# Router logits, places and masked context in quadrants of 32 result rows, in a fused cross-attention and mixture-of-experts kernel on one core

## The chip, the core and the metric

The kernel runs on one core of a Trainium2 chip. A core has a matrix engine (TensorE, PE in the profile, with its weight loads shown apart as PEld), a vector engine (DVE), a scalar engine (ACT), a general engine (POOL) and a queue processor (SP) that issues transfers. Matrix products land in PSUM, from where DVE or ACT copies them on. The metric is device time in microseconds (us) of one execution; lower is better. All data are 32-bit floats.

## What is computed

The input is 64 batches of 128 tokens of width 128, and for each batch a context of 77 rows of width 96. Two residual blocks follow each other:

```python
x = x + tanh(g_xattn[0]) * xattn(layernorm(x), ctx, mask)   # 16 heads of 8, softmax over 77 context rows
x = x + tanh(g_ffn[0])   * ffn(layernorm(x))

# ffn: 8 experts, 2 of them per token
gate_scores = softmax(x @ Wg)                      # Wg: 128 x 8, the router
topk_scores, topk_idx = top_k(gate_scores, 2)
topk_scores = topk_scores / (topk_scores.sum(-1) + 1e-8)
fused = gate * sigmoid(gate) * value               # gate = x @ W11[e], value = x @ W12[e], 128 -> 256
expert_out = fused @ W2[e]                         # 256 -> 128
out = sum of topk_scores * expert_out over the two experts
```

The kernel doesn't compute all eight experts for every token. It sorts the tokens by expert: each token's row is written to DRAM at a place that belongs to its expert, and the expert stage then works through tiles of 128 rows with one expert each.

## The kernel before

**Attention.** The 64 batches are taken in 16 groups of four (`G = 4`). A main loop runs over items `i`, one per batch: `scores` of batch `i`, `turn` (transposes of the score differences and their exponentials) of batch `i - 1`, `values` of a batch further on, `mix` (the sums over the context) of batch `i - 2`, `turn_last` of batch `i - 1`. Around these pieces each item has two slots, PRE (ahead of the scores) and POST (behind `turn_last`). The steps that belong to a whole group are placed in these slots by hand: the table `AT` gives each step's item relative to the group's first batch, and the order in which instructions are written is the order on PE, ACT, DVE and POOL (`tc.manual_schedule`). SP's transfers are outside of it.

Three of these steps are touched by the change:

- `context_t` (L520, at item -7, POST): per batch the product of the context (77 rows x 96 columns, the stationary operand) with `sel`, a 77 x 77 matrix that masks rows out. The result `pc` has 96 rows and 4 x 77 columns. ACT copies it out as `cT` (L527) and partly as `czs` (L529). On PE it stands between `tl` (the transposes of `turn_last`, L895) and `pt_a`, the transposes of the normalised tokens (L389), which the next item's scores (`sc`, L860) follow.
- `logits` (L635, at item 13, PRE): per batch the product of the transposed tokens (128 x 128, stationary) with `wg` (128 x 8). The result `pg` has 128 rows and 4 x 8 columns. DVE reads it twice, as `gm` and `gp` (L644, L646).
- `places` (L698, at item 17, PRE): two products accumulated in one result `pp` of 128 x 32: `earlier` (a triangle of ones, 128 x 128, stationary) with the group's choices `both`, and `ones` (128 x 128, stationary) with the running counts. They give each token its place within its expert's region. DVE turns this into `place` (L708), `at`, `to` and `dest` (L717), and POOL uses `dest` in the group's eight dispatches (L722): indirect transfers of 128 rows each, two of them directly after the item's scores and the others in the next items' slots. Items 13 and 17 differ by one group, so `places` of group g - 1 and `logits` of group g come in the same slot, one behind the other, ahead of that item's scores. In most groups `pk`, the keys product of a later group (L544), stands just before them.

Results of most products share a ring of three PSUM buffers (`product`, L382). A product that takes a buffer must wait until its last result has been read. As the program is built, in the items with places and logits the places take the buffer of `po` (the mix, read by ACT as `os` and `lz`, L921 and L922), the logits that of `tl` (read by ACT at L900), the first transposes of `turn` (`tp`, L882) that of the places, the second transposes that of the logits, and the mix that of `pk` (read by ACT as `kb`, L550, four times).

**Quadrants in the code.** A product whose result is a range of 32 rows, starting at 0, 32, 64 or 96, uses 32 columns of its stationary operand. `values` (L833, L845) and `mix` (L914) are written that way already, because their operands come in blocks of 32; all the other products in the kernel, but for the scores, have results of full height. In the profile a shape such as `128*32` is the part of the array that an instruction uses: contraction rows by stationary columns.

**Expert stage.** After the last item, 142 tiles of 128 rows run through `load`, `turned` (L1025), `up` (L1035), `flip` (L1050) and `down` (L1058), and POOL writes every tile's results back by an indirect transfer (L1066). The tokens are in two parts (groups 0 to 11, and 12 to 15); the first part's tiles start when its dispatches have landed, and what is left of the second part's steps, logits of groups 14 and 15 and places of groups 13 to 15 among them, is run between these tiles, with the ring reduced to two buffers. Last come the sums of both experts' results and the stores.

Of the kernel before, what the change touches and what calls it, by code (L numbers as in the profile page):

```python
# [21 lines left out]
G = 4  # L22
# [14 lines left out]
def tile_gated_xattn_moe(  # L37
# [17 lines left out]
    nc = tc.nc  # L55
    B, S, D = x.shape
    M, CD = context.shape[1:]
    E, _, I = W11.shape
    P = 128
# [26 lines left out]
    def part_of(g):  # L86
        return parts[g >= SPLIT]
# [8 lines left out]
    cs = {}  # L96
# [18 lines left out]
    wg = wts.tile([D, E], F32, name="wg")  # L115
# [12 lines left out]
    def load_expert(k):  # L128
# [48 lines left out]
    earlier = const.tile([P, P], F32, name="earlier")  # L177
    nc.gpsimd.memset(earlier, 1.0)
    nc.gpsimd.affine_select(
        earlier, earlier, pattern=[[1, P]], compare_op=ALU.is_gt, fill=0.0,  # L180
        base=0, channel_multiplier=-1,
    )
    ones = const.tile([P, P], F32, name="ones")
# [32 lines left out]
    for q in range(NQ):  # L216
        for k in range(2):
            r = 32 * q + 16 * k
# [89 lines left out]
    with ExitStack() as ph:  # L308
# [73 lines left out]
        def product(shape, n):  # L382
            return ring[0].tile(shape, F32, tag="pr", name=n)
# [69 lines left out]
        def step(name):  # L453
            def add(f):
                STEP[name] = f
                TURN.setdefault(AT[name], []).append(name)
                return f

            return add
# [59 lines left out]
        @step("context_t")  # L519
        def context_t(gr, g):  # L520
            pc = product([CD, G, M], f"pc_{g}")
            for b in range(G):
                nc.tensor.matmul(  # L523
                    pc[:, b, :], cs[g][:, b, :], gr.sel[:, b, :], start=True, stop=True
                )
            gr.cT = a3.tile([CD, G, M], F32, tag="cT", name=f"cT_{g}")
            nc.scalar.copy(gr.cT, pc)  # L527
            gr.cz = czs[g % 3]
            nc.scalar.copy(gr.cz[:, :, 1, :ML], pc[:, :, JM:])  # L529
# [103 lines left out]
        @step("logits")  # L633
        def logits(gr, g):
            gr.pg = product(ge, f"pg_{g}")  # L635
            for b in range(G):
                nc.tensor.matmul(  # L637
                    gr.pg[:, b, :], gr.xT[:, b * S : (b + 1) * S], wg, start=True, stop=True
                )

        @step("less_max")
        def less_max(gr, g):
# [54 lines left out]
        @step("places")  # L697
        def places(gr, g):  # L698
            gr.pp = product(ge, f"pp_{g}")
            nc.tensor.matmul(gr.pp, earlier, gr.both, start=True, stop=False)  # L700
            pt = part_of(g)
            i = (g - pt.g0) * G
            nc.tensor.matmul(gr.pp, ones, pt.run[:, i : i + G], start=False, stop=True)

        @step("places_in")
        def places_in(gr, g):
# [263 lines left out]
        for i in range(NBT + 2):  # L970
# [10 lines left out]
            if 0 <= i - 2 < NBT:  # L981
                g, b = divmod(i - 2, G)
# [185 lines left out]
```

## Time and profile before

| | |
|---|---|
| median of 3 runs | 694.02 us (693.63 to 695.32) |
| the profiled execution | 692.33 us, of which 690.2 between its first and last instruction |
| mean granted TensorE clock | 0.981 |
| PE busy | 615.3 us (89% of the span), 7703 matmul records |
| weight loads (PEld) | 429.2 us (62%), 7703 records |
| DVE, ACT, POOL busy | 466.1, 392.9 and 442.0 us |

The products that the change touches, with the records of both kinds (an fp32 product that isn't a transpose is two matmul records and two loads):

| product | line | records | matmul busy us, mean ns | load busy us, mean ns |
|---|---|---|---|---|
| `pc`, context | L523 | 128 | 13.9, 253 | 13.4, 172 |
| `pg`, logits | L637 | 128 | 16.5, 255 | 15.6, 192 |
| `pp`, places, first | L700 | 32 | 5.0, 239 | 5.4, 189 |
| `pp`, places, second | L703 | 32 | 6.2, 276 | 4.9, 192 |
| `pv` by quadrants, 64 columns | L833 | 512 | 20.9, 236 | 10.3, 110 |
| `pv` by quadrants, 16 columns | L845 | 1024 | 19.3, 184 | 16.6, 115 |

How to read it: busy time is the union of the records' times, and the mean is that of one record, so where records overlap the mean times the count is more than the busy time. A timeline row gives the start and the length of a run of equal records, their number, and in brackets how long the engine was idle before it and what ended that. The ends of matmuls are modelled. Attention fills the first 380 us or so, the expert stage the rest.

### The profile page before, as it was taken

Reading aid. Unit: us, or ns where it says so; the run is one execution under the profiler, and the core shown is the slowest. Engines: PE = TensorE matmul, PEld = TensorE weight load, DVE = VectorE, ACT = ScalarE, POOL = GpSimd, SP = SyncE. Lnnn points to the kernel's source line nnn. Section 1 sums busy time; section 2 is a strip of 40 time slices with the busy share of each in tenths; the row PEclk is TensorE's granted clock in tenths of the full one; section 3 lists DMA queues with packets and bytes.
Section 4 is the critical chain, followed back from the end, with each engine's and each line's share of the span. In section 5 each row is a group of like instructions: output and inputs, shape, how many; then the busy total and the mean of one; then the engine's idle time right before and its main releaser. Section 6 shows DMA issues by size and latency. Waiting matters only on the chain.

```text
span 690.2 us, 21369 instructions
## 1 busy us (share of the span) xinstructions
PE 615.3 (89%) x7703; PEld 429.2 (62%) x7703; DVE 466.1 (68%) x1440; ACT 392.9 (57%) x1042; POOL 442.0 (64%) x769
## 2 busy tenths in 40 slices
PE   4799999999999999999988699999978999999770
PEld 3577777776776677676666266666555665656450
DVE  4758798788878887887797356465455454546673
ACT  3697888787877787787655433543432333333220
POOL 4411125577557755765565488888888888887671
PEclk9999999999999999999999899999999999999995
DMA  4493001111110100000110342222222313264666
GB/s 105 124 280 94 16 15 29 38 32 39 33 40 31 32 27 26 26 31 22 34 57 22 84 106 73 75 71 71 80 79 68 103 59 90 80 204 124 194 187 205
DMA packets 64510, 53.55 MB, mean 78 GB/s; under 512 B 14131, under 2 KB 58235, under 8 KB 64408
## 3 DMA queue, kind: packets, MB, share of 16 engines
q1 hardware_dynamic: 46424, 30.52, 16.5%
q0 software_dynamic: 8640, 17.06, 7.5%
q10 hardware_dynamic: 9344, 4.62, 2.4%
q8 instruction: 63, 1.03, 0.6%
q14 instruction: 39, 0.32, 0.2%
HBM read 28.88 MB, written 24.20 MB: 77 GB/s over the span
## 4 chain that ended last, share of the span: by engine, by line
PE 71%; DVE 9%; ACT 6%; issue 5%; POOL 5%; DMA 3%; another core or an unknown queue 1%; POOLq 0%; ACTq 0%; DVEq 0%; SPq 0%
PE pu L1035 16%; PE po L914 11%; PE tp L882 8%; PE pot L1058 7%; PE sc L860 5%; PE phh L1050 4%; PE ptt L1025 3%; PE tl L895 3%; POOL yb L1066 3%; PE pq L561 3%; PE py L584 2%; PE pc L523 2%; PE pg L637 2%; PE pv L833 2%; DVE x L1101 2%
## 5 line engine op out<-in xcount | busy, mean ns | idle before, releaser
L722 POOL DMA_INDIRECT xg<-rows,dest x128 | 127.1, 993 | 66.3 <-DVE gm L644 41.9
L1066 POOL DMA_INDIRECT yb<-y,xt x142 | 140.8, 992 | 41.4 <-issue 13.3
L1035 PE MATMUL pu<-wx,xTt 128*128 x284 | 153.7, 623 | 8.5 <-issue 7.6
L1041 ACT ACTIVATE sgt<-pu 128x256 f32<-128x256 f32 x142 | 54.5, 384 | 170.3 <-PE pu L1035 97.9
L1043 DVE TENSOR_TENSOR ht<-sgt,pu 128x256 f32<-128x256 f32 x142 | 59.6, 420 | 98.9 <-ACT sgt L1041 59.4
L869 DVE TENSOR_REDUCE mx<-sc 128x16 f32<-128x1232 f32 x64 | 91.6, 1431 | 22.4 <-PE sc L860 21.2
L1050 PEld LDWEIGHTS phh<-ident,ht 128*128 128x128 f32 x284 | 39.4, 141 | 79.6 <-issue 68.3
L1058 PE MATMUL pot<-wx,hTt 128*128 x568 | 87.0, 276 | 0.3 <-issue 0.3
L887 ACT ACTIVATE pT<-tp,drop 128x512 f32<-128x512 f32 x128 | 80.3, 677 | 9.9 <-PE tp L882 9.9
L872 DVE TENSOR_TENSOR pe<-sc,mx 128x1024 f32<-128x1024 f32 x64 | 78.4, 1224 | 2.2
L1058 PEld LDWEIGHTS pot<-wx,hTt 128*128 128x128 f32 x568 | 75.0, 192 | 0.4 <-issue 0.4
L914 PE MATMUL po<-pT,own 128*32 128x128 f32 x1536 | 66.9, 274 | 8.1 <-issue 7.8
L882 PEld LDWEIGHTS tp<-ident,pe 128*128 128x128 f32 x512 | 55.6, 142 | 27.9 <-issue 8.9
L882 PE MATMUL tp<-ident,pe 128*128 128x128 f32 x512 | 70.8, 282 | 0.9 <-ACT kb L550 0.6
L914 PE MATMUL po<-pT,va 128*32 128x128 f32 x1536 | 60.8, 274 | 2.3 <-issue 2.0
L1064 DVE TENSOR_SCALAR y<-pot,xt 128x128 f32<-128x128 f32 x142 | 49.0, 347 | 19.9 <-PE ptt L1025 8.5
L1052 ACT COPY hTt<-phh 128x256 f32<-128x256 f32 x142 | 52.3, 368 | 9.8 <-PE ptt L1025 5.5
L1050 PE MATMUL phh<-ident,ht 128*128 128x128 f32 x284 | 54.8, 275 | 3.1 <-ACT hTt L1052 1.9
L914 PEld LDWEIGHTS po<-pT,own 128*32 128x32 f32 x1536 | 46.2, 110 | 17.3 <-issue 17.1
L860 PE MATMUL sc<-kb,qT 32*128 32x308 f32 x512 | 52.5, 480 | 4.4 <-DVE pls L872 2.6
L365 POOL TENSOR_TENSOR rs_a<-rs_a,live 128x4 f32<-128x4 f32 x15 | 3.0, 199 | 81.9 <-ACT rs_a L362 74.1
L1035 PEld LDWEIGHTS pu<-wx,xTt 128*128 128x128 f32 x284 | 43.4, 193 | 19.0 <-issue 17.5
(167 smaller groups left out, 1109.9 us busy)
## 6 DMA issues: line engine op xcount, KB each, us to landing
xt<-xg SPq DMA_DIRECT2D x142, 66.0 KB
ys<-yb SPq DMA_DIRECT2D x16, 512.0 KB
out_dram<-x ACTq DMA_DIRECT2D x16, 256.0 KB
x<-in_x_dram SPq DMA_DIRECT2D x15, 256.0 KB
yb<-y,xt POOLq DMA_INDIRECT x142
wx<-in_L_ffn_W_dram SPq DMA_DIRECT2D x2, 1024.0 KB
xg<-rows,dest POOLq DMA_INDIRECT x128
xg<-empty SPq DMA_DIRECT2D x30, 66.0 KB
```

Source lines behind the costliest of these rows:

```text
L722: i = nc.gpsimd.indirect_dma_start(out=part_of(g).xg[:, :], out_offset=bass.IndirectOffsetOnAxis(ap=gr.dest[:, k, b : b + 1], axis=0), in_ ...
L860: nc.tensor.matmul(sc[:, q, :W], gr.qT[r, b * S : (b + 1) * S], gr.kb[r, b].rearrange("p h j -> p (h j)"), start=True, stop=True,)
L869: nc.vector.tensor_reduce(mx[:, :, :, 0], sv, AX.X, ALU.max)
L872: nc.vector.tensor_tensor(dst[:, :, :, : j1 - j0], sv[:, :, :, j0:j1], mx.to_broadcast([P, NQ, HQ, j1 - j0]), ALU.subtract,)
L882: nc.tensor.transpose(tp[:, u, :], pe[:, q + u // 2, 2 * (u % 2) : 2 * (u % 2) + 2].rearrange("p h j -> p (h j)"), ident,)
L887: nc.scalar.activation(pT[:, 2 * q : 2 * q + 4], tp, AF.Exp, bias=drop[:, 0, i : i + 1], scale=scale)
L914: nc.tensor.matmul(po[32 * q : 32 * q + 32, v, :], w, pT[:, 2 * q + c if c < 2 else 8 + q // 2, :], start=(c == 0), stop=(c == 2),)
L1035: nc.tensor.matmul(pu.rearrange("p j i -> p (j i)"), ti.xT, wxf[:, bass.ds(ti.e, 2 * I)], start=True, stop=True,)
L1043: nc.vector.tensor_tensor(ti.h.rearrange("p c i -> p (c i)"), sg, pu[:, 1], ALU.mult)
L1050: nc.tensor.transpose(pt[:, c], ti.h[:, c], ident)
L1058: nc.tensor.matmul(po, ti.hT[:, c], wxf[:, bass.ds(ti.e + w, D)], start=(c == 0), stop=(c == NC - 1),)
L1066: i = nc.gpsimd.indirect_dma_start(out=ti.pt.yb[:, :], out_offset=bass.IndirectOffsetOnAxis(ap=ti.x[:, D : D + 1].bitcast(I32), axis=0), i ...
```

## The change

The three steps are split by quadrants of 32 result rows: each product becomes three (context, 96 rows) or four (logits, places) products, each with 32 columns of the same stationary operand and with the whole of the same moving operand. The places keep their accumulation in two steps, `earlier` first for all four quadrants, then `ones`. What is computed, the results' buffers, and all other instructions and their order stay as they are.

```diff
         def context_t(gr, g):
             pc = product([CD, G, M], f"pc_{g}")
             for b in range(G):
-                nc.tensor.matmul(
-                    pc[:, b, :], cs[g][:, b, :], gr.sel[:, b, :], start=True, stop=True
-                )
+                for r in range(0, CD, 32):
+                    nc.tensor.matmul(
+                        pc[r : r + 32, b, :], cs[g][:, b, r : r + 32], gr.sel[:, b, :],
+                        start=True, stop=True,
+                    )
...
         def logits(gr, g):
             gr.pg = product(ge, f"pg_{g}")
             for b in range(G):
-                nc.tensor.matmul(
-                    gr.pg[:, b, :], gr.xT[:, b * S : (b + 1) * S], wg, start=True, stop=True
-                )
+                for r in range(0, P, 32):
+                    nc.tensor.matmul(
+                        gr.pg[r : r + 32, b, :], gr.xT[:, b * S + r : b * S + r + 32], wg,
+                        start=True, stop=True,
+                    )
...
         def places(gr, g):
             gr.pp = product(ge, f"pp_{g}")
-            nc.tensor.matmul(gr.pp, earlier, gr.both, start=True, stop=False)
             pt = part_of(g)
             i = (g - pt.g0) * G
-            nc.tensor.matmul(gr.pp, ones, pt.run[:, i : i + G], start=False, stop=True)
+            for k, (w, of) in enumerate(((earlier, gr.both), (ones, pt.run[:, i : i + G]))):
+                for r in range(0, P, 32):
+                    nc.tensor.matmul(
+                        gr.pp[r : r + 32], w[:, r : r + 32], of, start=(k == 0), stop=(k == 1)
+                    )
```

## The prediction

> **What bounds the kernel now.** I read the page first: busy time in 40 slices, then the chain of work that ended last.
>
> ```profile
> PE   4799999999999999999988699999978999999770
> ...
> POOL 4411125577557755765565488888888888887671
> ...
> PE 71%; DVE 9%; ACT 6%; issue 5%; POOL 5%; DMA 3%; another core or an unknown queue 1%; POOLq 0%; ACTq 0%; DVEq 0%; SPq 0%
> ```
>
> TensorE is full from start to end and holds 71% of the chain, so time taken from it ought to count. Whether it does depends on who is next. So I read one group of four batches as a timeline, engine by engine: group 7's logits and what follows. PE first:
>
> ```profile
> 242.00 0.44 PE L895 MATMUL tl<-ident,pls 128*128 128x128 f32 x2
> 242.28 0.68 PE L544 MATMUL pk<-cT,wk 96*128 96x308 f32 x2
> 242.80 0.30 PE L700 MATMUL pp<-both,earlier 128*128 128x32 f32 x2
> 242.94 0.39 PE L703 MATMUL pp<-run,ones 128*128 128x32 f32 x2
> 243.16 1.04 PE L637 MATMUL pg<-wg,xT_f 128*128 128x8 f32 x8
> 244.13 0.80 PE L860 MATMUL sc<-kb,qT 32*128 32x308 f32 x8
> 244.86 1.09 PE L882 MATMUL tp<-ident,pe 128*128 128x128 f32 x8
> 245.89 0.32 PE L833 MATMUL pv<-wv,cT 96*32 96x64 f32 x8
> 246.02 0.29 PE L845 MATMUL pv<-wv,czs 96*32 96x16 f32 x16
> ...
> 247.57 0.90 PE L914 MATMUL po<-pT,own 128*32 128x128 f32 x22 [0.28 <-issue]
> ...
> 248.67 0.83 PE L523 MATMUL pc<-sel,c 77*96 77x77 f32 x8
> ...
> 251.88 0.84 PE L914 MATMUL po<-pT,va 128*32 128x128 f32 x24
> 252.54 0.84 PE L914 MATMUL po<-pT,own 128*32 128x128 f32 x24
> ```
>
> Places, logits and scores follow each other without a hole. The mix at 251.88 takes 1.50 us (to 253.38); the one that starts at 246.15 takes 2.32, with a hole before 247.57. The same stretch on POOL, then on DVE, then on ACT:
>
> ```profile
> 244.77 0.96 POOL L722 DMA_INDIRECT xg<-rows,dest  x1 [3.36 <-DVE gm L644]
> ...
> 246.28 0.97 POOL L722 DMA_INDIRECT xg<-rows,dest  x1 [0.16 <-issue]
> ...
> 248.45 1.00 POOL L722 DMA_INDIRECT xg<-rows,dest  x1 [0.17 <-issue]
> ```
>
> ```profile
> 243.37 0.19 DVE L708 TENSOR_TENSOR place<-pp,region 128x32 f32<-128x32 f32 x1 [1.61 <-PE pp L703]
> ...
> 244.62 0.19 DVE L646 TENSOR_TENSOR gp<-pg,gm 128x32 f32<-128x32 f32 x1
> ```
>
> ```profile
> 249.80 0.41 ACT L527 COPY cT<-pc 96x308 f32<-96x308 f32 x1 [0.45 <-PE pc L523]
> ```
>
> PE's hole ends 0.32 us after POOL's second dispatch (246.28 + 0.97 = 247.25). ACT's copy of the context starts 0.35 after the third (249.45), though its product ended at 249.50; in groups 3 to 5, with no dispatch running, it starts 0.04 after its product. From 249.80 ACT is busy without a break to the end of the exponentials at 253.79, and the next queries product starts at 253.84. So through each group from 2 to 9 a second chain runs beside PE's: places, DVE's dest, three dispatches on POOL, ACT, queries.
>
> **The change part by part.** Each fp32 product is two records (64 logits products, x128). Logits go from 64 products to 256, context from 64 to 192, places from 32 to 128: 416 more, 832 more matmul records on 7703 and as many loads. Order and buffers of all other instructions stay, on every engine. The instruction queue (63 packets, 0.6% of the DMA engines) gets a tenth more to fetch, hidden under the DMA share of 0.10 between 84 and 341 us.
>
> *Pace.* Full height: eight logits records in 1.04, one lasting 0.256, are (1.04 - 0.256) / 7 = 112 ns apart. By quadrants: the 16-column product has 16 in 0.29, one 0.183, so 7.1 ns apart, 28 for a pass of four quadrants. With 64 columns (0.32, x8, 0.243) it is 11 and 44; with 128 (0.84, x24, 0.273) 25 and 99. I take 28 for logits (8 columns), 36 for places (32, between 28 and 44), 60 for context (77, between 44 and 99). The far bound for all three is 99, at which the logits gain nothing.
>
> The Trainium skill, "TensorE: Matmul & The Clock Gate" (section "Wait — 56ns, not 53.3ns?"), says that starts of matmuls never come closer than about 25 ns. By that a logits block would take 32 x 25 = 800 ns, nearly the 892 of now, and the change would give back its gain; the row of 7.1 ns says otherwise here. The same page (Part 3, "The mechanism") says that a weight load overlaps running products only when its row group differs, which column quadrants don't offer: loads of 0.11 one by one would make a block 3.5 us and the kernel some 42 us slower. The loads of the 16-column product (16 in 0.25, each 0.113) overlap, so I don't count it.
>
> *A change of tile shape.* In the rows, weights of another shape load only 0.07 before the modelled end of the last product: po ends at 242.08, tl loads at 242.00. And the second record after a change comes 0.17 after the first (tl: 0.44 - 0.27), not 0.11. The change adds one such switch ahead of places and two around each context block.
>
> *Places, group 7.* Loads started at 242.62; now they wait for pk's end, 242.96 - 0.07 = 242.89. Four passes, the first 0.08, end the last record at about 243.26, not 243.33: DVE's place 0.08 earlier, bounds 0 and 0.13. In group 1, where ACT's lz holds the loads to 105.2 in any case, it is 0.28.
>
> *Logits, group 7.* 243.08 + 8 x 28 ns, last record to 243.50, scores loading at 243.43, not 244.13: 0.70 off PE. Bound: 0.
>
> *Who is late next.* In the built program the first transposes (tp) take the buffer of pp, the second that of pg, and the mix that of pk. The second must wait for DVE's gp: 244.81 - 0.08 + 0.06 = 244.79 where they started at 245.30. So 0.5 of the 0.7 is left, and the mix could start at 245.65. But the hole follows the dispatches, and these follow dest: their ends move 0.08. PE may leave the mix up to 0.5 earlier; ACT's cT, behind the third dispatch, moves 0.08, and with it the queries. So a group gains 0.08; if cT followed PE it would be 0.5 to 0.6.
>
> *Context, group by group.* Now 8 records at 82 ns, (0.83 - 0.253) / 7, loads running on from tl. Then: 0.09 for the switch, first pass 0.08, seven of 60, 0.09 again and 0.06 for the transposes' unready weights: the product ends within 0.03 of now, what follows is 0.15 later. In groups 4 to 15 ACT, which sets the queries, covers it: PE's load for pq stands at 253.84 where tl left off at 253.59, and cT has 0.26 (249.80 against 249.54). Without this cover it costs 0.15, and more if PE has not its 48 context instructions at hand when the third dispatch begins: then the rest comes 0.33 after its end, about 0.35 late. In groups 1 to 3 nothing covers it: +0.45.
>
> *The sum*, against this execution's 692.33 us (span 690.2, 2.1 around it; the median of the runs, 694.02, is 1.7 above):
> - group 0 (no places beside it, no dispatch yet): -0.5 (0 to -0.6);
> - group 1: -0.28; groups 2 to 10: 9 x -0.08 = -0.7;
> - group 11 (333.8 us): no context behind it, four dispatches in its mix of 3.47 us, DVE idle 2.39 until its scores at 340.64. The mix starts 0.5 earlier and more of it is done before they begin: -1.0 (0 to -2.0);
> - groups 12 and 13 lie under DVE's own chain (341 to 369 us): 0;
> - expert stage: two logits (421.15, 477.6 us), 0.89 now, then 0.22 + 0.09 + 0.09 + 0.06 and a first pass: -0.35 each, of which I count -0.5 in all; three places there, 0.45 now, as long then: 0;
> - context: +0.45.
> Together -2.5, so 689.8, and 691.5 against the median.
>
> **Rivals.**
> 1. *ACT's cT waits for PE, not for POOL.* For it: the profile itself names pc as the releaser. And in group 6 cT starts 0.04 after pc although a dispatch ended just then. Against: the steady 0.34 to 0.40 after the third dispatch in groups 7 to 14. Then 8 groups (context 7 to 14) gain 0.5 to 0.6 more, 4.5 in all: 687.0.
> 2. *PE's gain is hidden wherever it arises*: group 11's mix still ends with its dispatches and the expert stage waits for POOL (busy 227 of 278 us there). The dest terms alone remain, -1.0, and context's +0.45: 693.5.
> 3. *Slower: PE runs out of context instructions under POOL's third dispatch.* For it: in the mix at 246.28 some 35 records start before the hole, and tl, context and transposes together now need 58 behind such a dispatch. Against: up to 85 start under one that follows a pause, and the mix leaves early. It decides as soon as the last context record starts after 249.4. Price 0.35 to 0.6 in 9 groups, 4.5, with half of the 3.0 of gains and context's 0.45: 4.5 - 1.5 + 0.45 = +3.5: 697.5.
> 4. *The quadrants run one after another.* With three quadrants or eight columns no row of this kernel shows it; the four-quadrant rows speak against it. Context would go from 0.67 to 24 x 60 ns = 1.4 us plus switches, 15 x 0.9, with logits unchanged: 708.
>
> **How the numbers follow.** Chances: my sum 0.40, rival 1 0.17, rival 2 0.17, rival 3 0.21, rival 4 0.05. A measurement of this kernel can tell 0.3% (2.1 us) from no change. My sum with its bounds is faster in 0.27 of its 0.40, else the same; rival 1 faster; rival 2 the same; rivals 3 and 4 slower. That makes 0.44, 0.30, 0.26. The sum's own range is 689.5 to 693.5; with rivals 1 to 3 it becomes 686.5 to 698.
>
> **What would show it.** Right: logits records 7 ns apart, scores 0.7 earlier after pp; the second tp ending its wait with gp; mixes in groups 2 to 10 still ending about 0.6 to 1.0 after a dispatch; cT still 0.35 behind the third; pq 0.05 behind pT. Wrong: records of pg at 25 ns or more apart, context blocks with a hole inside, cT 0.04 after pc, or a group period (now 22.9 us, 243.16 - 220.2) that moves by more than 0.2.

## The result, and the profile after

| | before | changed |
|---|---|---|
| median of 11 runs each | 694.02 us (691.08 to 695.82) | 692.48 us (690.75 to 693.99) |
| ratio, 95% interval | | 0.9975 (0.9959 to 0.9991) |
| span of the profiled execution | 690.2 us | 691.2 us |
| matmul records, PE busy | 7703, 615.3 us | 8535, 613.5 us |
| weight loads, busy | 7703, 429.2 us | 8535, 414.6 us |

The changed kernel is 1.7 us faster (0.6 to 2.8): the interval excludes zero, but the gain is under the 0.3% (2.1 us) below which the prediction calls two kernels the same. The two profiled executions stand the other way round, by 1.0 us. They are single executions, so what follows compares stretches of them and leaves the judgement of the whole to the medians.

First, the page of the changed kernel: the busy tenths in 40 slices, and the chain that ended last.

```profile
PE   4799999999999999999988798998899999989770
...
POOL 4411125576657665755565487888888888887672
...
PE 73%; DVE 8%; issue 7%; ACT 7%; POOL 2%; DMA 1%; SPq 0%; ACTq 0%; POOLq 0%; DVEq 0%
```

TensorE is as full as it was, and "issue", time in which nothing that the profile shows is waited for, went from 5% to 7% of the chain. Second, the groups of the changed kernel by line and shape (busy us, mean ns of one record).

```profile
L524 PE MATMUL pc<-sel,c 77*32 77x77 f32 x384 | 12.7, 239 | 0.3 <-issue 0.3
L640 PE MATMUL pg<-wg,xT_f 128*32 128x8 f32 x512 | 7.3, 179 | 0.4 <-ACT lz L929 0.4
L708 PE MATMUL pp<-both,earlier 128*32 128x32 f32 x128 | 4.3, 206 | 0.0
L708 PE MATMUL pp<-run,ones 128*32 128x32 f32 x128 | 4.3, 196 | 0.3 <-issue 0.3
```

The logits keep PE busy 7.3 us instead of 16.5, the places 8.6 instead of 11.2, the context 12.7 instead of 13.9: 13 us of busy time less, of which 1.7 us are seen in the median. PE's busy time as a whole fell by 1.8 us only: records of neighbouring groups overlap (before the change the groups' busy times add up to 771 us, and PE is busy for 615), so busy time taken from a group isn't time taken from PE. Third, the timeline of group 7, PE with the instructions of the other engines that matter to it. All stands a little over 0.7 us earlier here than before the change, so read distances, not clock times.

```profile
241.53 0.69 PE L546 MATMUL pk<-cT,wk 96*128 96x308 f32 x2
242.14 0.27 PE L708 MATMUL pp<-both,earlier 128*32 128x32 f32 x8
242.23 0.25 PE L708 MATMUL pp<-run,ones 128*32 128x32 f32 x8
242.29 0.46 PE L640 MATMUL pg<-wg,xT_f 128*32 128x8 f32 x32
242.54 0.19 DVE L715 TENSOR_TENSOR place<-pp,region 128x32 f32<-128x32 f32 x1 [1.38 <-PE pp L708]
242.68 0.80 PE L867 MATMUL sc<-kb,qT 32*128 32x308 f32 x8
243.41 1.35 PE L889 MATMUL tp<-ident,pe 128*128 128x128 f32 x8
243.80 0.19 DVE L650 TENSOR_TENSOR gp<-pg,gm 128x32 f32<-128x32 f32 x1
243.95 0.96 POOL L729 DMA_INDIRECT xg<-rows,dest  x1 [3.27 <-DVE gm L648]
244.11 0.42 PEld L889 LDWEIGHTS tp<-ident,pe 128*128 128x128 f32 x4 [0.28 <-PE tp L889]
244.95 0.84 PE L921 MATMUL po<-pT,va 128*32 128x128 f32 x24
245.46 0.97 POOL L729 DMA_INDIRECT xg<-rows,dest  x1 [0.16 <-issue]
245.61 0.89 PE L921 MATMUL po<-pT,own 128*32 128x128 f32 x10
246.80 0.66 PE L921 MATMUL po<-pT,own 128*32 128x128 f32 x14 [0.30 <-issue]
247.39 0.44 PE L902 MATMUL tl<-ident,pls 128*128 128x128 f32 x2
247.63 1.00 POOL L729 DMA_INDIRECT xg<-rows,dest  x1 [0.16 <-issue]
247.76 0.74 PE L524 MATMUL pc<-sel,c 77*32 77x77 f32 x24
248.43 0.66 PE L389 MATMUL pt_a<-ident,xn 128*128 128x128 f32 x4
249.01 0.80 PE L867 MATMUL sc<-kb,qT 32*128 32x308 f32 x8
249.08 0.41 ACT L529 COPY cT<-pc 96x308 f32<-96x308 f32 x1 [0.74 <-PE pt_a L389]
```

The distances, before and after:

| distance in group 7 | before | after |
|---|---|---|
| `pk`'s end to the first `pp` record | -0.16 | -0.08 |
| `pk`'s end to DVE's `place` | 0.41 | 0.32 |
| first `pp` to first `sc` | 1.33 | 0.54 |
| first `pp` to the mix | 3.35 | 2.81 |
| second dispatch's end to the end of PE's hole | 0.32 | 0.37 |
| third dispatch's end to ACT's `cT` | 0.35 | 0.45 |
| first `pp` to `cT` | 7.00 | 6.94 |

The scores come 0.79 earlier and the mix 0.54, and at `cT` 0.06 is left of it. The 0.5 us are spent in the hole before 246.80: 34 of the mix's 48 records start ahead of it, where it was 26, and still the mix lasts 2.51 us instead of 2.32, because the hole ends with the dispatch. The second transposes load 0.12 after DVE's `gp` ends (243.99 to 244.11): the wait the prediction named. The mix ends 1.03 after its dispatch, where it was 1.22.

### The profile page after: what moved, and what is told of

Read it like the earlier page. It is cut to its first block, busy times and chain, and to the rows that moved or that the text cites. A ratio compares the mean times of both kernels' runs of the same rounds, so it can differ in the third digit from the quotient of the medians.

```text
span 691.2 us, 23033 instructions
## 1 busy us (share of the span) xinstructions
PE 613.5 (89%) x8535; PEld 414.6 (60%) x8535; DVE 465.7 (67%) x1440; ACT 394.0 (57%) x1042; POOL 441.5 (64%) x769
## 4 chain that ended last, share of the span: by engine, by line
PE 73%; DVE 8%; issue 7%; ACT 7%; POOL 2%; DMA 1%; SPq 0%; ACTq 0%; POOLq 0%; DVEq 0%
PE pu L1042 18%; PE po L921 12%; PE tp L889 8%; PE pot L1065 8%; PE sc L867 6%; PE phh L1057 4%; PE ptt L1032 3%; PE tl L902 3%; PE pq L563 2%; PE py L586 2%; DVE x L1108 2%; PE pv L840 2%; ACT pT L894 2%; DVE mx L876 1%; DVE pe L879 1%
## 5 line engine op out<-in xcount | busy, mean ns | idle before, releaser
L1042 PE MATMUL pu<-wx,xTt 128*128 x284 | 155.8, 631 | 9.0 <-issue 7.5
L921 PE MATMUL po<-pT,own 128*32 128x128 f32 x1536 | 68.4, 276 | 7.9 <-issue 7.2
L889 PE MATMUL tp<-ident,pe 128*128 128x128 f32 x512 | 72.7, 282 | 1.8 <-ACT kb L552 0.6
L889 PEld LDWEIGHTS tp<-ident,pe 128*128 128x128 f32 x512 | 55.3, 142 | 30.9 <-issue 10.4
L921 PE MATMUL po<-pT,va 128*32 128x128 f32 x1536 | 57.7, 275 | 3.4 <-DVE st L793 2.1
L921 PEld LDWEIGHTS po<-pT,own 128*32 128x32 f32 x1536 | 47.6, 110 | 17.5 <-issue 17.1
L1032 PE MATMUL ptt<-ident,xt 128*128 128x128 f32 x142 | 41.7, 293 | 16.9 <-issue 10.2
```

Source lines behind the costliest of these rows:

```text
L889: nc.tensor.transpose(tp[:, u, :], pe[:, q + u // 2, 2 * (u % 2) : 2 * (u % 2) + 2].rearrange("p h j -> p (h j)"), ident,)
L921: nc.tensor.matmul(po[32 * q : 32 * q + 32, v, :], w, pT[:, 2 * q + c if c < 2 else 8 + q // 2, :], start=(c == 0), stop=(c == 2),)
L1032: nc.tensor.transpose(pt, ti.x[:, :D], ident)
L1042: nc.tensor.matmul(pu.rearrange("p j i -> p (j i)"), ti.xT, wxf[:, bass.ds(ti.e, 2 * I)], start=True, stop=True,)
```

## The experiments

The runs fell on several chips, and the time of one and the same kernel differs by 8% between them, so each ratio is against the kernel before on the same chip. The traces show what differs. On one chip (709 us) there are holes in the mixes of groups 2 to 10 as in the first comparison; on three others (655 to 657 us) those mixes last 1.50 us, without a hole but for single ones (1.6 to 2.0), though POOL's records of the dispatches are as long as elsewhere (0.973 to 0.977 us in the median of every trace). I call them chips with and without holes. "Held" in the table marks the kernels whose dispatches wait for the mix, described below.

| run | logits | places | context | holes | time, us | before, us | ratio, 95% interval |
|---|---|---|---|---|---|---|---|
| e1_logits | quadrants | | | no | 649.95 | 656.55 | 0.9902 (0.9869 to 0.9934) |
| e2_places | | quadrants | | no | 654.36 | 656.55 | 0.9966 (0.9944 to 0.9988) |
| e3_context | | | quadrants | no | 658.50 | 656.55 | 1.0033 (1.0011 to 1.0055) |
| e4_logits_places | quadrants | quadrants | | no | 647.38 | 656.55 | 0.9860 (0.9829 to 0.9891) |
| e5_hold_after | quadrants | quadrants | quadrants | no, held | 655.98 | 654.70 | 1.0012 (0.9990 to 1.0033) |
| e6_hold_before | | | | no, held | 663.24 | 654.70 | 1.0115 (1.0084 to 1.0146) |
| e7_after | quadrants | quadrants | quadrants | yes | 708.75 | 708.98 | 1.0006 (0.9985 to 1.0027) |
| e8_before | | | | yes | 707.13 | 708.98 | one run |
| e9_logits_places | quadrants | quadrants | | yes | 704.30 | 708.98 | 0.9941 (0.9917 to 0.9965) |
| e10_after | quadrants | quadrants | quadrants | no | 650.76 | 655.72 | 0.9925 (0.9899 to 0.9951) |
| e11_context | | | quadrants | no | 658.54 | 655.72 | 1.0031 (1.0008 to 1.0054) |
| e12_hold_after | quadrants | quadrants | quadrants | no, held | 655.76 | 655.72 | 1.0005 (0.9990 to 1.0020) |

The theory under test: the gain of logits and places is real and is swallowed in groups 2 to 10, because a chain over three POOL dispatches sets `cT`. The rivals: `cT` waits for PE; PE's gain is hidden for another reason; the context's many instructions cost what the rest brings.

**One part at a time.** Each kernel is the kernel before with one hunk of the change's diff, or two. For the logits alone:

```diff
             for b in range(G):
-                nc.tensor.matmul(
-                    gr.pg[:, b, :], gr.xT[:, b * S : (b + 1) * S], wg, start=True, stop=True
-                )
+                for r in range(0, P, 32):
+                    nc.tensor.matmul(
+                        gr.pg[r : r + 32, b, :], gr.xT[:, b * S + r : b * S + r + 32], wg,
+                        start=True, stop=True,
+                    )
```

> Only the logits are in quadrants; places and context as before. Theory (each group's period is set by the chain places, dest, dispatches, ACT's context copy, queries, so that PE's gain in the logits is absorbed): the copy cT stays where it is, group period unchanged between groups 2 and 10, and only group 0 (-0.5) and the expert stage (-0.5) gain: -0.5 to -1.2 us against before, 0.998 to 0.9995. Rival (PE sets the pace, so every logits block counts with the 0.6 us that it loses): 12 blocks in attention, -6 to -7 us, 0.990.

> Only the places are in quadrants. Theory: DVE's place starts 0.05 to 0.1 earlier in each of groups 2 to 10, 0.2 to 0.3 in group 1, and the whole period moves with it: -0.7 to -1.2 us, about 0.9985. Rival (PE sets the pace): 0.15 us of PE time per group less the switch of tile shape, within 0.2 us in all, 1.000.

> Only the context is in quadrants. Theory: what follows the context block is 0.15 us later, which counts in groups 1 to 3 alone, plus one hole in group 15's block under a dispatch (0.6 us): +0.4 to +1.2 us, 1.0005 to 1.002. Rival (the three context instructions more per product run dry under POOL's third dispatch in every group): +3 to +5 us, 1.005. Rival (PE sets the pace): +0.15 x 15 = +2.2 us, 1.003.

> Logits and places in quadrants, context as before. Theory: the sum of the two, -1.5 to -3.0 us, 0.9965, that is 0.5 to 1.2 us under the full change. If the context's quadrants are free or a gain, it equals the full change or is slower than it.

Measured, by the ratios: -6.4, -2.2, +2.2 and -9.2 us. The sizes of logits and context missed what the theory gave, since on this chip the absorber isn't there: the mixes last 1.50 us and `cT` starts 0.04 after its product (0.06 with the context in quadrants). Both met the size of the rival that has PE set the pace (0.990 and 1.003), so here `cT` waits for PE. (For the context the rival with holes in its blocks, 1.005, lies within the interval, but in the trace each block from group 1 on takes 0.74 us, without a hole.) The places decide less: the theory's 0.9985 lies within their interval, that rival's 1.000 doesn't. The period of a group, from the scores of batch 21 to those of batch 57 divided by nine, is 20.88 us with the context alone, 20.64 with the places, 20.36 with the logits, 20.13 with logits and places. So the logits on top of the places take off 0.51 and the places on top of the logits 0.23. The kernel before left no trace on a chip without holes, so what a part alone takes off its period can't be read; by the ratios, -0.98% and -0.34% make -1.32%, against -1.40% measured.

**Hold the dispatches behind the mix.** The dispatches of groups 0 to 9, and the first two of group 10, get a copy on POOL that reads one column of the mix's result, and three of each group's eight go to a later slot. What is computed stays.

```diff
-            "dispatch10": (18, PRE),
+            "dispatch10": (18, POST),
...
-            "dispatch20": (19, PRE),
+            "dispatch20": (19, POST),
...
-            "dispatch30": (19, POST),
+            "dispatch30": (20, POST),
...
             def f(gr, g):
+                t = G * g + 17 + b - 2
+                if t < 56:
+                    nc.gpsimd.tensor_copy(spare_w[:, 0:1], groups[t // G].os[:, t % G, 0:1])
                 nc.gpsimd.memset(spare_w, 0.0)
```

> The changed kernel, with the dispatches of groups 0 to 10 held: each waits on POOL until ACT has copied the mix of its item (a one-column copy from os ahead of the spacer), and they stand two by two behind items 17 to 20. Theory (a running dispatch keeps PE and ACT from getting instructions): no dispatch runs under a mix any more, so mixes of 2.3 to 3.0 us become 1.50; per group two mixes lose 0.9 and 1.3 us of holes, part of which ACT's chain takes back: 10 groups x 0.5 to 1.8, -5 to -18 us against before, unless POOL's later work is now late. Rival (the holes have another cause, such as the instruction fetch itself): mixes keep their holes at the same places and the time stays within 2 us or gets worse by POOL's waits.

> The kernel before, with the dispatches held as in the run before this one. Theory: with the dispatches out of the mix the absorber is gone, so the quadrants' gain should show: this kernel is slower than the held changed one by more than the 1.5 us between the two unheld ones, 3 to 6 us. Rival (the gain of the logits is absorbed by ACT's keys copies or DVE rather than by the dispatches): the difference stays 1.5 us.

Measured: 655.98 and 663.24 us, on a chip without holes. There was no hole to take away, and holding only costs: 1.2% for the kernel before, and 5.0 us or 0.8% for the changed one, taken on the one chip that ran it with and without (650.76 in e10_after, 655.76 in e12_hold_after). The 1.0012 of e5_hold_after is against the kernel before and holds this cost and the change's gain. That the dispatch under the mix is what makes the hole stays untested by this. The difference of the two, 7.3 us where 3 to 6 were expected, says what the change is worth in that order of work: 1.00 us of a period (20.76 against 21.76).

**Both kernels, and logits with places, on one chip.** It was one with holes. The first of the three is the changed kernel and the second the kernel before, both as they are; the third is e4's.

> The changed kernel itself, unedited, once more beside the kernel before. In the traces of the runs so far no mix has the holes that both first traces have (mixes 1.50 us throughout, cT 0.04 us after its product), and all times are some 38 us lower. Theory (the dispatches' holes set each group's period and absorb the gain): where the traces have no holes, the change gives the sum of its three parts, -0.98% -0.34% +0.33%, some -1.0% or -6.5 us; where they have holes, -0.25% again. Rival (the parts don't add up, the whole change is worth -0.25% anywhere): -1.6 us in both.

> The kernel before, unedited, for its trace beside the last one's. Theory: without holes its period between groups 2 and 10 is set by PE (the logits item's scores follow the logits without a wait of another engine), about 20.7 us per group; with holes 22.9 us.

> Logits and places in quadrants, context as before, once more. Without holes: 0.986 of the kernel before and 0.4% to 0.5% under the full change. With holes: the full change's -0.25% and what the context costs in groups 1 to 3 and 15, -1.0 us more, 0.996.

Measured: 708.75, 707.13 and 704.30 us, the last ratio clear of the first's. The whole change is worth nothing that can be told on this chip (the expected 0.9975 lies just outside of 0.9985 to 1.0027), logits and places alone 0.6%; by the two ratios the context costs 1.0006 / 0.9941, 0.65% or 4.6 us (roughly 2 to 7 by their intervals). A group's period in the kernel before is 23.1 us there, where 22.9 was expected. The timelines show how. The third dispatch, with the context and copy of group 11, in the changed kernel, then in the one without context quadrants:

```profile
225.56 0.44 PE L902 MATMUL tl<-ident,pls 128*128 128x128 f32 x2
225.75 1.00 POOL L729 DMA_INDIRECT xg<-rows,dest  x1 [0.16 <-issue]
225.93 0.74 PE L524 MATMUL pc<-sel,c 77*32 77x77 f32 x24
226.04 0.47 ACT L907 ACTIVATE pT<-tl,drop 128x256 f32<-128x256 f32 x1
227.25 0.41 ACT L529 COPY cT<-pc 96x308 f32<-96x308 f32 x1 [0.74 <-PE pt_a L389]
```

```profile
222.60 0.44 PE L900 MATMUL tl<-ident,pls 128*128 128x128 f32 x2
222.80 1.00 POOL L727 DMA_INDIRECT xg<-rows,dest  x1 [0.17 <-issue]
222.88 0.83 PE L523 MATMUL pc<-sel,c 77*96 77x77 f32 x8
223.08 0.47 ACT L905 ACTIVATE pT<-tl,drop 128x256 f32<-128x256 f32 x1
223.74 0.41 ACT L527 COPY cT<-pc 96x308 f32<-96x308 f32 x1 [0.19 <-PE pc L523]
```

In both, the context's product ends 1.11 us after `tl` starts (226.67 and 223.71), a little before the dispatch ends, and ACT's copy before, `pT`, stands 0.29 and 0.28 after the dispatch's start. With quadrants `cT` starts 0.50 after the dispatch's end and 0.58 after its product; with full height it starts 0.03 after its product, while the dispatch still runs. The same split holds in seven of the eight groups from 7 to 14 (the exception is group 9 of the full-height kernel). So between the scores of batches 20 and 52 the kernel without context quadrants gains 0.35 us a group on the kernel before, the changed kernel 0.03. In the kernel before (e8_before) `cT` also stands behind the dispatch, 0.41 to 0.44 after its end, but there the product itself ends 0.08 to 0.20 after it. What changes sides is thus the pair: PE earlier and few context instructions frees `cT`; PE earlier and many doesn't. Whether PE's signal or ACT's instruction is late isn't shown.

**Once more, with the context alone and the held kernel.** The edits are those above.

> The changed kernel without any edit, once more, beside its two parts below. The places and the logits take time off TensorE in every group; how much of it arrives depends, by the runs before this one, on whether the mixes of groups 2 to 10 have a hole behind a dispatch (2.4 to 3.0 us) or none (1.50 us). Theory of the absorber: if this kernel's mixes and the kernel before's have holes in this run, the ratio is between 0.996 and 1.001, as in both such runs so far; if they have none, the parts' ratios of that kind (0.990, 0.997 and 1.003) give 0.990 in all, and the range is 0.987 to 0.993. Rival, that the differing times have to do with something else than the holes: the ratio is near 0.998 either way.

> Only the context is written by quadrants; logits and places stay as they were. Without holes this part measured 1.0033. If the mixes have holes in this run, the theory is that the context's 48 instructions hold ACT's copy cT another 0.3 us in groups 7 to 14 and that nothing is gained elsewhere: 8 x 0.3 = 2.4 us, plus 0.45 for groups 1 to 3 and 0.6 for group 15, 3.5 us or +0.5%, and the gaps from product to copy are 0.5 to 0.7 us in groups 7 to 14, against 0.25 to 0.35 before. Rival, that the context costs the same 0.15 us per group in both cases and cT's wait is the dispatch's alone: +0.3% or less, gaps of 0.25 to 0.35. If there are no holes: 1.001 to 1.006 again.

> The changed kernel with the dispatches of groups 0 to 10 held behind the mix, by a copy on POOL of one column of the mix's result, and three of them one slot later; the numbers computed stay the same. If this run's plain kernels have holes: the mixes of groups 2 to 10 should last 1.5 us here, without a hole. Theory that the dispatch under the mix is what starves TensorE: the period of a group falls from about 22.9 us to about 21, worth 9 x 1.9 = 17 us less what the later dispatches cost at group 11 and the expert stage's start (some 5 us), so about -12 us, ratio near 0.983. Rival, that the hole only moves to what now runs under the dispatch (values, transposes): the period stays above 22.5 us and the ratio is 0.995 to 1.01. If there are no holes in the plain kernels: 0.999 to 1.003, as in the run of that kind.

Measured: 0.9925, 1.0031 and 1.0005, on a chip without holes: all three within what the theory gave for that case, the first one outside of its rival's 0.998 (0.9899 to 0.9951). One group of the changed kernel on this chip, all engines:

```profile
210.04 0.84 PE L921 MATMUL po<-pT,va 128*32 128x128 f32 x24
210.55 0.98 POOL L729 DMA_INDIRECT xg<-rows,dest  x1 [0.17 <-issue]
210.70 0.84 PE L921 MATMUL po<-pT,own 128*32 128x128 f32 x24
211.47 0.44 PE L902 MATMUL tl<-ident,pls 128*128 128x128 f32 x2
211.83 0.74 PE L524 MATMUL pc<-sel,c 77*32 77x77 f32 x24
...
212.63 0.41 ACT L529 COPY cT<-pc 96x308 f32<-96x308 f32 x1
212.73 1.00 POOL L729 DMA_INDIRECT xg<-rows,dest  x1 [0.17 <-issue]
```

The mix ends at 211.54 with a dispatch of 0.98 us inside it, and `cT` starts 0.06 after its product (212.57), ahead of the third dispatch. The period is 20.27 us against 20.88 with the context alone: 0.61 us a group for logits and places, where the whole change left 0.06 at `cT` in group 7 of the first comparison. Against the 20.13 of logits and places without the context's quadrants, these cost 0.14 a group. The whole change's gain is swallowed in both comparisons that have holes and in none without. That the holes swallow it is argued from this and from the mix's end, which stays with the dispatch; taking the holes away would show it, and the held kernel met none again.

**The version that beats both.** Logits and places by quadrants with the context in full height: 0.986 without holes, 0.9941 with them.

## Why the prediction was right, and where it was not

It said 691.5 us and -2.5; the runs say 692.48 and -1.7 (0.6 to 2.8 less). Its likeliest case, that TensorE's gain is real but meets a chain over the dispatches, is what the traces with holes show, as far as they can: the waits end behind dispatches, but no run took the dispatches away. Step by step:

- *Pace.* Right in kind. Logits records start (0.46 - 0.179) / 31 = 9.1 ns apart, not 7.1: 36 a pass instead of 28. Places: (0.27 - 0.206) / 7 = 9.1, 37 a pass (36 said). Context: (0.74 - 0.239) / 23 = 21.8, 65 a pass (60 said). The floor of 25 ns between starts and the rule that loads overlap only across row groups, both from the Trainium skill ("TensorE: Matmul & The Clock Gate", "Wait — 56ns, not 53.3ns?" and Part 3, "The mechanism"), don't hold for column quadrants here: 32 loads of 111 ns stand in 0.40 us.
- *Shape switch and places.* Right: `pp` starts 0.08 before `pk`'s end (0.07 said), `place` comes 0.09 earlier (0.08 said).
- *Logits and who is late next.* Right: from the places to the scores 0.79 less (0.70 said for the logits, and a little for the places), 0.54 left at the mix because the second transposes wait for `gp` (0.5 said). The mix ends 1.03 after its dispatch (0.6 to 1.0 said), where it was 1.22, so against the dispatch PE gains 0.19 there.
- *Groups 2 to 10.* Right where the whole change is on a chip with holes: DVE's `place` moves from -0.33 us in group 1 to -0.87 in group 8, 0.08 a group (0.08 said); in the later pair with holes it is -0.12 and -0.61, 0.07 a group. But the reason given was too firm. `cT` isn't behind the third dispatch whatever the context's form: with full height it gets free and a group gains 0.35.
- *Group 0.* Right: 0.61 (0.5 said), from the scores of its item. *Group 1* was mis-sized: `place` gains 0.94 from group 0 to group 1 (0.28 said). The mix of batch 15, the first with dispatches in it, lasts 1.61 us instead of 2.38, which accounts for most of it; in the later pair with holes it is 1.62 instead of 2.44.
- *Context.* The failed term of the sum. Said: +0.45 in groups 1 to 3, the rest covered. The local figures are right: the product ends 1.11 after `tl` starts in either form, and what follows is 0.15 later (1.62 against 1.47 from `tl` to the scores). Without holes nothing covers this, 15 x 0.15 = 2.25 us, and +2.2 (0.7 to 3.6) and +2.0 (0.5 to 3.5) were measured. With holes it is 4.6 us, of which the trace of e7_after against e9_logits_places shows 2.3 us between the scores of batches 21 and 52, by the late `cT`, and 1.6 us ahead of those of batch 8. The first comparison has the second piece too: at the scores of batch 8, ahead of all logits and places, the changed kernel is 1.16 us late, where 0.45 was said for the whole run. (The cover read off for the other groups, 253.84 against 253.59, is 0.33 and not 0.25 in the rows: the loads of `tl` end at 253.31 + 0.20 = 253.51.)
- Those 1.6 us hold a piece that wasn't in the sum at all. In six of the seven traces with context quadrants the mix of batch 2 has a hole (2.2 to 2.8 us instead of 1.50); in none of the seven without. From the changed kernel, timeline of PE:

```profile
44.31 0.82 PE L921 MATMUL po<-pT,va 128*32 128x128 f32 x19
46.02 0.31 PE L921 MATMUL po<-pT,va 128*32 128x128 f32 x3 [0.89 <-issue]
```

  Idle 0.89 us, released by nothing that the profile shows, while SP's transfers of the first inputs still run. Why it comes with the added instructions wasn't settled.
- *Group 11.* Mis-sized: -1.0 said. The mix ends at 339.95 instead of 340.27, 0.32 earlier, and 0.18 of this is there already when the group's `pk` starts (332.75 instead of 332.93), so the group itself brings 0.14. Its mix starts 0.6 earlier, at 336.20, and meets the same dispatches (three run under it, not four):

```profile
336.20 0.84 PE L921 MATMUL po<-pT,va 128*32 128x128 f32 x24
336.71 0.96 POOL L729 DMA_INDIRECT xg<-rows,dest  x1 [0.17 <-issue]
336.86 0.86 PE L921 MATMUL po<-pT,own 128*32 128x128 f32 x9
338.06 0.46 PE L921 MATMUL po<-pT,own 128*32 128x128 f32 x7 [0.34 <-issue]
338.22 0.97 POOL L729 DMA_INDIRECT xg<-rows,dest  x1 [0.17 <-issue]
338.82 0.44 PE L921 MATMUL po<-pT,own 128*32 128x128 f32 x6 [0.30 <-issue]
339.56 0.39 PE L921 MATMUL po<-pT,own 128*32 128x128 f32 x2 [0.30 <-issue]
```

- *Expert stage.* -0.5 said. In both pairs with holes the changed kernel's scores of the last batch are earlier (-0.2 and -1.3 us against the kernel before) and its end is later (+1.0 and +1.5 by the spans), and without context quadrants -6.7 became -4.4. So some 1 to 3 us were given back there (1.2, 2.8 and 2.3), in one execution each. The clock records offer a cause that isn't shown: from the last batch's scores on, the granted clock is 0.5 for 30.9 us in the changed kernel's trace and for 26.4 in the one before, and 1.0 otherwise; in the later traces it is 0.5 for 38.7 us and, without context quadrants, 40.4, against 30.3. The `pu` products there (L1035 before) keep PE busy 2.1, 3.2 and 2.3 us longer. It needn't come from the change: the executions of the kernel before on the chip of the later traces have mean clocks from 0.968 to 0.983. In the six unheld traces without holes the stage lasts 306.8 to 308.0 us whichever parts are in quadrants, so 0.5 us can't be told there.
- *Rival 3* (PE runs out of context instructions under a dispatch): the hole inside the block, as it was put, appears in one group of the first comparison, the last of the attention.

```profile
315.53 0.33 PE L524 MATMUL pc<-sel,c 77*32 77x77 f32 x5
316.17 0.66 PE L524 MATMUL pc<-sel,c 77*32 77x77 f32 x19 [0.31 <-issue]
```

  Five records start, then a hole, then the other 19: the block lasts 1.30 us instead of 0.74. `cT` starts 1.92 after this product (0.44 before the change), and the changed kernel, 1.37 us ahead at the scores of batch 54, is 0.19 ahead at the next. In groups 7 to 14 the blocks are whole, and in e7_after the last one is, too. Its direction was still the better half of the story: the context's instructions take back what logits and places bring, by the late `cT`. *Rival 1* holds without holes, and with them as soon as the context has full height. *Rival 2* is seen at group 11 and perhaps in the expert stage. *Rival 4* falls.

That the sum came out near the truth is luck in part, because two errors met: on the chip with holes where the parts were measured apart, logits and places were worth 4.2 us (2.5 to 5.9) where the sum has 3.0, and the context cost ten times its term. The whole change gave +0.4 us there (-1.1 to +1.9), not the sum's -2.5.

## What to carry to other kernels

Quadrants pay where the moving operand is narrow: 8 columns went from 0.89 to 0.3 us, while 77 columns gained nothing on TensorE and cost two shape switches. Before counting a gain, ask what ends the next wait in that stage, and ask it again for each part alone: two parts with a gain hid one that should have been left out. And where a wait has no releaser in the profile, look whether it is there on another chip before building on it.

## What the runs showed of the hardware that was not expected

- The kernel before took 655 to 657 us on three chips, 694 in the first comparison and 709 on another chip. For the changed kernel's traces at 709 and 651 us, 30 of the 58 us between them arise before the last batch's scores (371.1 against 340.9 us) and 28 in the expert stage. Most of the first part lies where the holes are: a group's period is 23.06 us in the one and 20.27 in the other, 9 x 2.79 = 25 us, although POOL's records of the transfers last 0.977 and 0.975 us. Why one chip has the holes and another hasn't, and where the 28 us come from, stays open.
- Under such a transfer an ACT copy can start 0.03 us after its product or 0.58 after it, with the product's end at the same place, as the product was 8 records or 24 (15 of 16 blocks of groups 7 to 14). That goes with the holes, too: on a chip without them (e3_context) the copy starts 0.06 after 24 records while the transfer runs.
